# Layers 2 and 3 of a four-layer image kernel: the nine taps of each depthwise convolution tile shared out in another way among TensorE, VectorE, ScalarE and GpSimd

## The chip, the core and the metric

The kernel runs on one core of a Trainium2 chip. The metric is the device time of one execution in microseconds (us); lower is better. Before the change it is 25110.91 us, the median of three runs (25106.78 to 25119.97).

## What is computed

Eight images of 64 x 64 pixels with 192 channels go through four layers. Layer 0 is a state-space block with two depthwise convolutions, layer 1 a selective scan in four directions, and layers 2 and 3 are the same small block, which is the part that the change touches:

```
def _L2_conv_ref(x, w, b):            # layer 3 is the same with its own w and b
    out = jax.lax.conv_general_dilated(x, w, window_strides=(1, 1), padding='SAME', ...,
                                       dimension_numbers=('NHWC', 'HWIO', 'NHWC'), feature_group_count=C)
    return out + b
...
def _gn(v, G=32, eps=1e-5):
    ...
    m = jnp.mean(g, axis=(1, 2, 4), keepdims=True)
    s = jnp.var(g, axis=(1, 2, 4), keepdims=True)
    return ((g - m) / jnp.sqrt(s + eps)).reshape(v.shape)
```

Each of these layers normalises its input over groups of six channels of an image, runs a depthwise 3 x 3 convolution over it (nine taps, one weight for each tap and channel), adds a bias, and adds the result to the input. All arithmetic is float32.

## The kernel before

The program runs in three parts, one after another: layer 0 (function `layer0`), layer 1 (`layer1_in` and `layer1_scan`), and `tail`, which holds the end of layer 1 and layers 2 and 3. Data between the parts lies in DRAM. `tail` is the only part that changes.

**Tiling.** Channels lie on partitions, 192 of them as two groups (`ct`) of 96. The 4096 pixels of an image are cut into eight strips of eight rows, 512 pixels each. The unit of a convolution is a tile: one strip of one channel group, 96 x 512, so there are 16 tiles for each image and layer and 256 in the kernel. A tile's input, with one more row above and below, is loaded into the tile `x2` or `x3` (`load_rows`, L1249).

**Four threads.** `tail` is written as four generators, and `together` (L74) goes round them, running each up to its next `yield`. The order in which this writes instructions is the order of every engine's queue; nothing is reordered later.

- `sums` (L1138) loads the four direction outputs of a strip (`yin`, by SyncE's DMA queue, `fetch`, L1129) and adds them: L1142 and L1146 on VectorE, L1143 on GpSimd. Then it takes row statistics (L1151, L1152, L1154), a reciprocal root (L92 to L97, with a load of the activation table, L1156), and normalises on ScalarE (L1161).
- `project` (L1168) transposes a strip on TensorE (L1177, evicted by L1179), multiplies it by a gate (matmuls L1183, Silu L1191 with its table load, product L1193), projects it (matmuls L1201), adds the residual (L1203), takes statistics (L1204) and stores the strip as `x2`. ScalarE normalises its input (L695).
- `all_convolutions(2)` runs layer 2 and stores `x3`, and `all_convolutions(3)` runs layer 3 and stores the output. Layer 2 of an image needs the statistics of the whole image, so it starts when the eight strips of the projection are done, beside the projection of the next image; layer 3 lies another image behind. `affine` (L1210) makes the weights and biases of an image: the normalisation is folded into them, so that the centre tap also holds the residual's one, and `edge` corrects the first and the last pixel of each row, where a tap would fall outside the image.

**One tile before** (`convolve`, L1260). TensorE multiplies the input by five diagonal matrices, for taps 1, 4 and 7 (the centre column) and 3 and 5, into one PSUM bank (L1282). ScalarE evicts the bank with the bias into `y` in SBUF (L1292). VectorE adds the edge corrections (L1296, L1297) and the other four taps, one instruction each, multiplying `x` by the weight and adding to `y`, all in SBUF (L1303). For layer 2, VectorE then takes statistics (L1313) and the strip goes to `x3`. For layer 3, `turn` (L1319) transposes the strip on TensorE (L1329), ScalarE copies it (L1331), and it goes out; this is done after the first eviction of the next strip. The eight PSUM banks are two for transposes (`tp`), three for the projection (`mm`) and three for convolutions (`cv`).

Of the kernel before, what the change touches and what calls it, by code (L numbers as in the profile page):

```python
# [10 lines left out]
AF = mybir.ActivationFunctionType  # L11
ALU = mybir.AluOpType
# [3 lines left out]
B, H, W, C = 8, 64, 64, 192  # L16
L = H * W
CP, CT = 96, 2
# [7 lines left out]
NJ = 512  # L26
NCH = L // NJ
# [644 lines left out]
def layers123(ctx: ExitStack, tc, a, dr, x1, mv1, out, cst):  # L672
# [416 lines left out]
def tail(ctx: ExitStack, tc, a, load, w_in, normed, yk, x2, x3, out, cst):  # L1089


    nc = tc.nc
    ident, grp = cst[0], cst[4]
    IDC = ident[:CP, :CP]
    R, NB = NJ // W, NJ // 128
    wp = ctx.enter_context(tc.tile_pool(name="wt", bufs=1))
    pool = ctx.enter_context(tc.tile_pool(name="t1", bufs=2))
    psum = ctx.enter_context(tc.tile_pool(name="pt1", bufs=1, space=PSUM))

    def bank(tag):  # L1100
        return mk(psum, [128, NJ], tag, bufs={"tp": 2, "mm": 3, "cv": 3}[tag])

    onw, onb = load("onw", [DP, DT]), load("onb", [DP, DT])
    w_out = load("w_out1", [DP, DT, C])
    zero = mk(wp, [CP, W], "zero")
    nc.vector.memset(zero, 0.0)
    TAPS = (1, 4, 7, 3, 5)
    base = {}
    for i in (2, 3):
        w, bt = mk(wp, [CP, CT, 9], f"w{i}"), mk(wp, [CP, CT], f"b{i}")  # L1110
        nc.sync.dma_start(w, a[f"L{i}_w"])
        nc.sync.dma_start(bt, a[f"L{i}_b"])
        dg, ws = mk(wp, [CP, CT, len(TAPS), CP], f"dg{i}"), mk(wp, [CP, CT, 3], f"ws{i}")
        for ct in range(CT):
            for j, tap in enumerate(TAPS):
                nc.vector.tensor_scalar(dg[:, ct, j, :], IDC, w[:, ct, tap : tap + 1], None, ALU.mult)
# [2 lines left out]
            nc.vector.tensor_tensor(ws[:, ct, :], ws[:, ct, :], w[:, ct, 6:9], ALU.add)  # L1119
        base[i] = w, bt, dg, ws  # L1120
    strips = [(b, r) for b in range(B) for r in range(NCH)]
    yin, rows, halo, stats, par = {}, {}, {}, {}, {}
    done = {"sums": 0, "x2": 0, "x3": 0}

    def at(s):
        return 0 <= s < len(strips)
# [41 lines left out]
    def project(s):  # L1168
# [5 lines left out]
        for o in range(DT):  # L1174
            pt = bank("tp")
            for t in range(NB):
                nc.tensor.transpose(pt[:, t * 128 : (t + 1) * 128], v[:, t, o * 128 : (o + 1) * 128], ident)  # L1177
            yield
            nc.scalar.activation(yn[:, o, :], pt, AF.Identity, bias=onb[:, o : o + 1], scale=onw[:, o : o + 1])  # L1179
        for o in range(DT):  # L1180
            ps = bank("mm")
            for ct in range(CT):
                nc.tensor.matmul(  # L1183
                    ps,
                    w_in[:, ct, DIN + o * 128 : DIN + (o + 1) * 128],
                    gx[:, ct, :],
                    start=ct == 0,
                    stop=ct == CT - 1,
                )
# [20 lines left out]
    def affine(i, b):  # L1210
# [24 lines left out]
        wi, edge = mk(pool, [CP, CT, 9], f"wi{i}"), mk(pool, [CP, CT, 3], f"edge{i}")  # L1235
        dgi = mk(pool, [CP, CT, len(TAPS), CP], f"dgi{i}")
        for ct in range(CT):
# [11 lines left out]
    def load_rows(i, s):  # L1249

        if not at(s):
            return
        b, r = strips[s]
        t = halo[i, s] = mk(pool, [CP, CT, (R + 2) * W], f"x{i}")
        lo, hi = max(0, r * R - 1), min(H, (r + 1) * R + 1)
        d0 = lo - (r * R - 1)
        src = (x2 if i == 2 else x3)[b]
        nc.sync.dma_start(t[:, :, d0 * W : (d0 + hi - lo) * W], src[:, :, lo * W : hi * W])

    def convolve(i, s, before=None):  # L1260


        b, r = strips[s]
        gm, wi, edge, dgi, cb = par[i]
        x, y = halo.pop((i, s)), mk(pool, [CP, CT, NJ], f"y{i}")
        if i == 2 and r == 0:
            stats[3, b] = mk(pool, [CP, CT, NCH, 6], "st3")
        for ct in range(CT):
            for edge_row, at_row in ((0, 0), (NCH - 1, (R + 1) * W)):
                if r == edge_row:  # L1270
                    nc.scalar.activation(  # L1271
                        x[:, ct, at_row : at_row + W], zero, AF.Identity, bias=gm[:, ct : ct + 1]
                    )
        for ct in range(CT):
            ps = bank("cv")[:CP]
            sv = x[:, ct, :].rearrange("p (h w) -> p h w", w=W)
            pv = ps.rearrange("p (h w) -> p h w", w=W)
            yv = y[:, ct, :].rearrange("p (h w) -> p h w", w=W)
            for j, tap in enumerate(TAPS):
                dy, dx = tap // 3, tap % 3 - 1  # L1280
                w0, w1 = max(0, -dx), W - max(0, dx)
                nc.tensor.matmul(  # L1282
                    pv[:, :, w0:w1],
                    dgi[:, ct, j, :],
                    sv[:, dy : dy + R, w0 + dx : w1 + dx],
                    start=j == 0,
                    stop=j == len(TAPS) - 1,
                    skip_group_check=True,
                )
                if j % 2:  # L1290
                    yield
            nc.scalar.activation(y[:, ct, :], ps, AF.Identity, bias=cb[:, ct : ct + 1])  # L1292
            yield
            if ct == 0 and before is not None:
                yield from turn(*before)
            nc.vector.tensor_scalar(yv[:, :, 0:1], yv[:, :, 0:1], edge[:, ct, 0:1], None, ALU.add)  # L1296
            nc.vector.tensor_scalar(yv[:, :, W - 1 : W], yv[:, :, W - 1 : W], edge[:, ct, 2:3], None, ALU.add)  # L1297
            for tap in range(9):
                if tap in TAPS:
                    continue  # L1300
                dy, dx = tap // 3, tap % 3 - 1
                w0, w1 = max(0, -dx), W - max(0, dx)
                nc.vector.scalar_tensor_tensor(  # L1303
                    yv[:, :, w0:w1],
                    sv[:, dy : dy + R, w0 + dx : w1 + dx],
                    wi[:, ct, tap : tap + 1],
                    yv[:, :, w0:w1],
                    ALU.mult,
                    ALU.add,
                )  # L1310
                yield
            if i == 2:
                nc.vector.bn_stats(stats[3, b][:, ct, r, :], y[:, ct, :])  # L1313
        if i == 2:
            nc.sync.dma_start(x3[b][:, :, r * NJ : (r + 1) * NJ], y)
            done["x3"] = s + 1
        return y

    def turn(s, y):  # L1319

        b, r = strips[s]
        ot = mk(pool, [128, NB, C], "ot")
        for g in range(NB // 2):
            ps = bank("tp")
            for j in range(2):
                t = (2 * g + j) * 128
                for ct in range(CT):
                    c0 = j * C + ct * CP
                    nc.tensor.transpose(ps[:, c0 : c0 + CP], y[:, ct, t : t + 128], IDC)  # L1329
            yield  # L1330
            nc.scalar.copy(ot[:, 2 * g : 2 * g + 2, :], ps[:, 0 : 2 * C].rearrange("p (j c) -> p j c", j=2))  # L1331
        nc.sync.dma_start(out[b].rearrange("(g j p) c -> g p j c", p=128, j=NB)[r], ot)
# [15 lines left out]
            yield from project(s)  # L1348

    def all_convolutions(i):  # L1350
        before = None
        for s in range(n):
            b, r = strips[s]
            if r == 0:
                while done[f"x{i}"] < s + NCH:
                    yield
                load_rows(i, s)
                yield from affine(i, b)
            if r < NCH - 1:
                load_rows(i, s + 1)  # L1360
            y = yield from convolve(i, s, before)
            if i == 3:
                before = s, y
        if before:
            yield from turn(*before)
        yield

    with every_engine(tc):
        together(all_projections(), all_sums(), all_convolutions(2), all_convolutions(3))
# [83 lines left out]
```

## Time and profile before

| what | us |
| --- | --- |
| median of three runs (lowest to highest) | 25110.91 (25106.78 to 25119.97) |
| span of the profiled execution, first to last instruction | 25098.0 |
| of this, `tail`, from 22890 to the end | 2208 |
| PE busy over the whole span | 23784.2 (95%) |
| VectorE (DVE) busy | 22334.3 (89%) |
| ScalarE (ACT) busy | 20190.7 (80%) |
| GpSimd (POOL) busy | 17651.1 (70%) |

The profiler records one execution. Its page gives the span of that execution; the time of the same execution outside its span is not listed, so it is the 12.9 us between the span and the median of the runs that are taken for what lies around. Shares of busy time are averages over all parts; for a change in `tail`, the stages of `tail` have to be read by themselves. PE is TensorE's matmul stream and PEld its loading of weights, which overlaps it. "Idle before" is time in which an engine stood still ahead of an instruction, and the arrow names what ended it.

### The profile page before, as it was taken

To read this page: it belongs to the slowest core of one execution; us is meant where nothing else is said; L and a number is where in the kernel's file an instruction comes from. 1 tells how busy PE (TensorE), PEld (TensorE's weight loads), DVE (VectorE), ACT (ScalarE), POOL (GpSimd) and SP (SyncE) were. 2 spreads that over 40 slices of the span, in tenths; PEclk is the share of its full clock that TensorE was granted. 3 is DMA by queue.
4 is the path that set the end of the run, shared out by engine and by line. 5 is a ranking of instruction groups with operands and counts; after the bars stand their busy time and mean duration, and the time that the engine had idled before them with its cause. 6 is when DMAs were issued, how large, how long until landed. Compare 5 with 4: busy or idle time off the path is not lost.

```text
span 25098.0 us, 445961 instructions
## 1 busy us (share of the span) xinstructions
PE 23784.2 (95%) x156672; PEld 18458.1 (74%) x156672; DVE 22334.3 (89%) x26682; ACT 20190.7 (80%) x40488; POOL 17651.1 (70%) x18332
## 2 busy tenths in 40 slices
PE   8999999988899999999999999999999999998999
PEld 4444444445688888888888888888888888885333
DVE  6777777766799999999999999999999999998887
ACT  4555555544599999999999999999999999997443
POOL 2322322310399999999999999999999999995110
PEclk8888888899999999999999999999999999999999
DMA  1111111123333333333333333333333333335554
GB/s 59 47 43 46 46 47 43 38 70 114 110 100 95 96 101 95 95 103 95 95 101 97 95 99 98 95 97 100 95 95 104 95 95 102 95 95 157 170 175 122
DMA packets 1506272, 2337.12 MB, mean 93 GB/s; under 512 B 249997, under 2 KB 775949, under 8 KB 1504026
## 3 DMA queue, kind: packets, MB, share of 16 engines
q1 hardware_dynamic: 1496858, 2283.42, 31.5%
q8 instruction: 1236, 20.25, 0.3%
q0 software_dynamic: 7168, 25.17, 0.3%
q14 instruction: 1010, 8.27, 0.1%
HBM read 1847.54 MB, written 460.59 MB: 92 GB/s over the span
## 4 chain that ended last, share of the span: by engine, by line
PE 36%; ACT 31%; DVE 13%; POOL 13%; issue 6%; DMA 0%; POOLq 0%; SPq 0%; DVEq 0%; ACTq 0%
ACT dA L1003 13%; POOL hc L1053 11%; ACT sb L987 7%; PE pd L1009 6%; PE yt L942 5%; DVE h L1044 5%; ACT bd L987 4%; PE cv L1282 4%; PE y L592 3%; PE pd L1011 2%; PE mm L901 2%; PE fc L626 2%; PE y L519 1%; PE cv L774 1%; PE tp L564 1%
## 5 line engine op out<-in xcount | busy, mean ns | idle before, releaser
L1053 POOL TENSOR_TENSOR hc<-h,bc 128x512 f32<-128x512 f32 x12288 | 15431.9, 1289 | 475.6 <-DVE h L1044 341.2
L1044 DVE TENSOR_TENSOR_SCAN h<-dA,st,pd 128x512 f32<-128x512 f32 x10752 | 12949.5, 1262 | 530.1 <-PE pd L1009 374.4
L1003 ACT ACTIVATE dA<-dl,A_logs 128x512 f32<-128x512 f32 x12288 | 8817.1, 718 | 47.0 <-DVE h L1044 39.6
L942 PE MATMUL yt<-sq,hc 128*128 128x128 f32 x49152 | 7489.3, 275 | 200.1 <-POOL hc L1053 93.8
L1009 PE MATMUL pd<-bd,dut 128*128 128x128 f32 x49152 | 6581.4, 277 | 254.4 <-DVE h L1044 232.1
L1009 PEld LDWEIGHTS pd<-bd,dut 128*128 128x128 f32 x49152 | 5968.5, 192 | 609.9 <-PE yt L942 342.9
L942 PEld LDWEIGHTS yt<-sq,hc 128*128 128x128 f32 x49152 | 5669.7, 141 | 644.3 <-POOL hc L1053 624.4
L987 ACT ACTIVATE sb<-dut,xt 128x384 f32<-128x384 f32 x8192 | 4779.5, 609 | 1.1 <-DVE dut L928 1.0
L1011 PE MATMUL pd<-sq,sb 128*128 128x128 f32 x24576 | 3739.5, 275 | 8.5 <-DVE h L1044 0.4
L1011 PEld LDWEIGHTS pd<-sq,sb 128*128 128x128 f32 x24576 | 2823.6, 141 | 479.1 <-DVE dl L915 380.8
L987 ACT ACTIVATE bd<-sq,xt 128x128 f32<-128x128 f32 x8192 | 3026.3, 395 | 0.0
L1044 DVE TENSOR_TENSOR_SCAN h<-dA,pd 128x512 f32<-128x512 f32 x1536 | 1770.8, 1204 | 117.0 <-PE pd L1009 67.2
L1143 POOL TENSOR_TENSOR yin<-yin,yin 128x1536 f32<-128x1536 f32 x64 | 233.9, 3655 | 1635.1 <-DMA yin<-y 892.5
L1282 PE MATMUL cv<-x,dgi 96*96 96x512 f32 (+1 forms) x2560 | 1175.0, 595 | 9.3 <-ACT x L1271 9.1
L481 POOL TENSOR_TENSOR xdt<-xb,dtv 128x384 f32<-128x384 f32 x256 | 217.1, 848 | 1186.6 <-ACT xb L475 1186.6
L234 DVE SCALAR_TENSOR_TENSOR x<-xs,cpe_w,x 96x504 f32<-96x504 f32 (+1 forms) x1024 | 886.6, 866 | 31.8 <-ACT x L222 21.7
L784 DVE SCALAR_TENSOR_TENSOR u<-xa,conv_w,u 128x504 f32<-128x504 f32 x1152 | 850.1, 743 | 50.5 <-ACT u L776 12.5
L1282 PEld LDWEIGHTS cv<-x,dgi 96*96 96x96 f32 x2560 | 413.0, 164 | 638.2 <-issue 604.5
L901 PE MATMUL mm<-xs,w_dt 13*128 13x512 f32 x1536 | 863.0, 641 | 1.8 <-DVE dl L915 1.0
L1055 POOL COPY st<-h 128x3 f32<-128x3 f32 x4096 | 825.0, 201 | 0.0
L1303 DVE SCALAR_TENSOR_TENSOR y<-x,wi,y 96x504 f32<-96x504 f32 x1024 | 796.0, 796 | 17.7
L626 PE MATMUL fc<-ff,fc_w 128*96 128x512 f32 x1536 | 791.0, 621 | 2.7 <-DVE xo L629 2.7
(263 smaller groups left out, 26186.7 us busy)
## 6 DMA issues: line engine op xcount, KB each, us to landing
bc<-bcd SPq DMA_DIRECT2D x4096, 256.0 KB
yin<-y SPq DMA_DIRECT2D x256, 768.0 KB
csb<-csd SPq DMA_DIRECT2D x256, 384.0 KB
dut<-ut SPq DMA_DIRECT2D x128, 768.0 KB
y<-ys SPq DMA_DIRECT2D x128, 768.0 KB
dut<-ut SPq DMA_DIRECT2D x256, 384.0 KB
y<-ys SPq DMA_DIRECT2D x256, 384.0 KB
xt<-x1d SPq DMA_DIRECT2D x128, 384.0 KB
```

What stands on the lines that cost most here:

```text
L234: nc.vector.scalar_tensor_tensor(d[:, :, w0:w1], s[:, dy : dy + R, w0 + dx : w1 + dx], w[:, ct, tap : tap + 1], d[:, :, w0:w1], ALU.mult, ...
L626: nc.tensor.matmul(ps, f2w[:, o, ct * CP : (ct + 1) * CP], ff[:, o, :], start=o == 0, stop=o == 5)
L784: nc.vector.scalar_tensor_tensor(uv[:, o, :, w0:w1], tv[:, o, dy : dy + R, w0 + dx : w1 + dx], cw[:, o, tap : tap + 1], uv[:, o, :, w0:w1] ...
L901: nc.tensor.matmul(ps, w_dt[:, k, o * 128 : (o + 1) * 128], made["xs"][0 : 1 + R1, :], start=True, stop=True)
L942: nc.tensor.matmul(yt[:, t * 128 : (t + 1) * 128], src[:, t * 128 : (t + 1) * 128], mat, is_transpose=mat is ident, start=first and t == 0 ...
L987: nc.scalar.activation(v, src, AF.Copy, scale=m["xt"][:, t, 1 + R1 + n : 2 + R1 + n])
L1003: nc.scalar.activation(dA, ready[s]["dl"][:, o, :], AF.Exp, scale=aneg[:, k, o, n : n + 1])
L1009: nc.tensor.matmul(dst, ready[s]["dut"][:, t, cols], brows[g, t], start=True, stop=True)
L1011: nc.tensor.transpose(dst, brows[g, t][:, cols], ident)
L1044: nc.vector.tensor_tensor_scan(h[:, o, rev], decay.pop(j)[:, rev], turned.pop(j)[:, rev], 0.0 if first else st[:, o, n : n + 1], ALU.mult, ...
L1053: nc.gpsimd.tensor_tensor(hc, h[:, o, :], held[g], ALU.mult)
L1282: nc.tensor.matmul(pv[:, :, w0:w1], dgi[:, ct, j, :], sv[:, dy : dy + R, w0 + dx : w1 + dx], start=j == 0, stop=j == len(TAPS) - 1, skip_g ...
```

## The change

The nine taps of a tile are split into three columns. The centre column (taps 1, 4, 7) stays on TensorE, now in full rows of 512, as three matmuls. The left column (0, 3, 6) is added by VectorE directly in PSUM (`side`), before the eviction. The right column (2, 5, 8) is made by ScalarE as three products in SBUF (`product`, six buffers for each layer), and after the eviction GpSimd adds the three products and the two edge corrections to `y` (`add`, and the two `tensor_scalar`).

A tile now goes through three steps in a line: `new` (matmuls and products), `old` (left side in PSUM, eviction, GpSimd's adds) and `older` (statistics and store, or the turn). Each call of `step` handles three successive tiles at once, one in each stage. When the input of the next image isn't there yet, and at the end, the line is emptied with two empty steps. The banks become two for the projection and four for convolutions, the input tiles get three buffers, and the diagonals of taps 3 and 5 are no longer made.

```diff
-        return mk(psum, [128, NJ], tag, bufs={"tp": 2, "mm": 3, "cv": 3}[tag])
+        return mk(psum, [128, NJ], tag, bufs={"tp": 2, "mm": 2, "cv": 4}[tag])
...
-    TAPS = (1, 4, 7, 3, 5)
+    TAPS, BY_DVE, BY_POOL = (1, 4, 7), (0, 3, 6), (2, 5, 8)
...
-        t = halo[i, s] = mk(pool, [CP, CT, (R + 2) * W], f"x{i}")
+        t = halo[i, s] = mk(pool, [CP, CT, (R + 2) * W], f"x{i}", bufs=3)
...
-    def convolve(i, s, before=None):
...
+    def column(m, j):
+        if j == 0:
+            m["ps"] = bank("cv")[:CP]
+        nc.tensor.matmul(
+            m["ps"], m["dg"][:, j, :], m["x"][:, j * W : j * W + NJ], start=j == 0, stop=j == 2, skip_group_check=True
+        )
+
+    def product(m, tap):
+        v, src = reach(m, tap)
+        t = m[tap] = mk(pool, [CP, NJ], f"prod{m['i']}", bufs=6)
+        nc.scalar.activation(by_rows(t)[:, :, v], src, AF.Copy, scale=m["w"][:, tap : tap + 1])
+
+    def side(m, tap):
+        v, src = reach(m, tap)
+        u = by_rows(m["ps"])[:, :, v]
+        nc.vector.scalar_tensor_tensor(u, src, m["w"][:, tap : tap + 1], u, ALU.mult, ALU.add)
+
+    def add(m, tap):
+        v, _ = reach(m, tap)
+        u = by_rows(m["y"])[:, :, v]
+        nc.gpsimd.tensor_tensor(u, u, by_rows(m[tap])[:, :, v], ALU.add)
+
+    def step(i, new, old, older):
+
+        for j in range(3):
+            if new:
+                column(new, j)
+                product(new, BY_POOL[j])
+            if j:
                 yield
+            if old:
+                side(old, BY_DVE[j])
+        yield
+        if older and i == 2:
...
+            nc.vector.bn_stats(stats[3, b][:, older["ct"], r, :], older["y"])
+            if older["ct"] == CT - 1:
+                nc.sync.dma_start(x3[b][:, :, r * NJ : (r + 1) * NJ], ys.pop((i, older["s"])))
+                done["x3"] = older["s"] + 1
+        if older and i == 3 and older["ct"] == CT - 1:
+            yield from turn(older["s"], ys.pop((i, older["s"])))
+        yield
+        if old:
...
+            nc.scalar.activation(old["y"], old["ps"], AF.Identity, bias=old["bias"])
+        yield
+        if old:
+            for tap in BY_POOL:
+                add(old, tap)
+            for at_col, e in ((0, 0), (W - 1, 2)):
+                v = by_rows(old["y"])[:, :, at_col : at_col + 1]
+                nc.gpsimd.tensor_scalar(v, v, old["edge"][:, e : e + 1], None, ALU.add)
+        yield
...
     def all_convolutions(i):
-        before = None
+        line = [None, None]
+
+        def push(m):
+            yield from step(i, m, *line)
+            line.insert(0, m)
+            line.pop()
+
         for s in range(n):
             b, r = strips[s]
             if r == 0:
+                if done[f"x{i}"] < s + NCH:
+                    for _ in range(2):
+                        yield from push(None)
                 while done[f"x{i}"] < s + NCH:
                     yield
...
-            y = yield from convolve(i, s, before)
-            if i == 3:
-                before = s, y
-        if before:
-            yield from turn(*before)
+            for ct in range(CT):
+                yield from push(begin(i, s, ct))
+        for _ in range(2):
+            yield from push(None)
         yield
```

More of the change, by code (lines that the diff above doesn't have):

```diff
@@ L1121, in tail @@
     strips = [(b, r) for b in range(B) for r in range(NCH)]
-    yin, rows, halo, stats, par = {}, {}, {}, {}, {}
+    yin, rows, halo, stats, par, ys = {}, {}, {}, {}, {}, {}
     done = {"sums": 0, "x2": 0, "x3": 0}
@@ L1258, in load_rows, with reach, by_rows, begin @@
         nc.sync.dma_start(t[:, :, d0 * W : (d0 + hi - lo) * W], src[:, :, lo * W : hi * W])
-    def convolve(i, s, before=None):
+    def reach(m, tap):
+        dy, dx = tap // 3, tap % 3 - 1
+        w0, w1 = max(0, -dx), W - max(0, dx)
+        return slice(w0, w1), by_rows(m["x"])[:, dy : dy + R, w0 + dx : w1 + dx]
+    def by_rows(v):
+        return v.rearrange("p (h w) -> p h w", w=W)
+    def begin(i, s, ct):
         b, r = strips[s]
         gm, wi, edge, dgi, cb = par[i]
[L1265 to L1294, printed above, removed]
-                yield from turn(*before)
[L1296 to L1310, printed above, removed]
-                yield
[L1312 to L1317, printed above, removed]
@@ new lines, in begin @@
+        m = {"i": i, "s": s, "ct": ct, "x": halo[i, s][:, ct, :], "w": wi[:, ct, :]}
+        m["edge"], m["bias"], m["dg"] = edge[:, ct, :], cb[:, ct : ct + 1], dgi[:, ct, :, :]
+        for edge_row, at_row in ((0, 0), (NCH - 1, (R + 1) * W)):
+            if r == edge_row:
+                nc.scalar.activation(m["x"][:, at_row : at_row + W], zero, AF.Identity, bias=gm[:, ct : ct + 1])
+        return m
+    def column(m, j):
[4 more added lines that the diff above has]
+        )
@@ new lines, in step @@
+    def step(i, new, old, older):
[4 more added lines that the diff above has]
+            if j:
+                yield
+            if old:
+                side(old, BY_DVE[j])
+        yield
+        if older and i == 2:
+            b, r = strips[older["s"]]
+            if r == 0 and older["ct"] == 0:
+                stats[3, b] = mk(pool, [CP, CT, NCH, 6], "st3")
+            nc.vector.bn_stats(stats[3, b][:, older["ct"], r, :], older["y"])
[6 more added lines that the diff above has]
+        if old:
+            s, ct = old["s"], old["ct"]
+            if ct == 0:
+                ys[i, s] = mk(pool, [CP, CT, NJ], f"y{i}")
+            old["y"] = ys[i, s][:, ct, :]
+            nc.scalar.activation(old["y"], old["ps"], AF.Identity, bias=old["bias"])
[7 more added lines that the diff above has]
+        yield
@@ L1360, in all_convolutions @@
                 load_rows(i, s + 1)
-            y = yield from convolve(i, s, before)
-            if i == 3:
-                before = s, y
-        if before:
-            yield from turn(*before)
+            for ct in range(CT):
+                yield from push(begin(i, s, ct))
+        for _ in range(2):
+            yield from push(None)
         yield
```

## The prediction

> **What bounds the kernel now.** I read the page first (who is busy), then the busy time by stage (where the change can act), then the groups and the single lines (what one instruction costs).
>
> ```profile
> span 25098.0 us, 445961 instructions
> ```
>
> Only the last 2208 us, the tail, hold the changed code. Cut by stage (columns: window, its length, busy time of PE, PEld, DVE, ACT and POOL with their instruction counts, granted clock, DMA share, GB/s):
>
> ```profile
> 22890.00:23077.00 187.00, 121.61 (x316) 55.00 (x314) 131.98 (x244) 97.59 (x145) 44.49 (x13) 0.80 0.72 232
> 23077.00:23290.00 213.00, 186.91 (x495) 78.43 (x495) 188.07 (x361) 103.11 (x164) 28.58 (x8) 0.94 0.66 198
> 23290.00:24870.00 1580.00, 1464.33 (x4070) 625.11 (x4068) 1343.81 (x2639) 705.36 (x1144) 161.84 (x45) 0.96 0.56 166
> 24870.00:25006.00 136.00, 128.77 (x336) 51.37 (x336) 104.47 (x209) 27.49 (x49) 0.00 (x0) 0.96 0.31 86
> 25006.00:25098.00 92.00, 78.90 (x234) 33.19 (x234) 56.31 (x116) 21.77 (x43) 0.00 (x0) 0.91 0.25 72
> ```
>
> Stages: A, projection of image 0 alone; B, image 1 beside convolution 2 of image 0; C, six images, each beside 32 convolution tiles; D, both convolutions without projection; E, convolution 3 of the last image alone. In C, PE is busy 1464 of 1580 and DVE 1344, while ACT has 705 and POOL 162. So PE sets the pace, 263 us an image, and the change moves work to the two engines with room.
>
> The groups (line, engine, operation, count | busy, mean ns of one | idle before):
>
> ```profile
> L1282 PE MATMUL cv<-x,dgi 96*96 96x512 f32 (+1 forms) x2560 | 1175.0, 595 | 9.3 <-ACT x L1271 9.1
> L1303 DVE SCALAR_TENSOR_TENSOR y<-x,wi,y 96x504 f32<-96x504 f32 x1024 | 796.0, 796 | 17.7
> L1292 ACT ACTIVATE y<-cv,acb 96x512 f32<-96x512 f32 x256 | 173.8, 681 | 712.3 <-PE cv L1282 694.8 <-issue 6.7 <-DVE y L1303 5.4
> ```
>
> A matmul is two passes (2560 for 1280); ten passes take 4.26 us in the chain of waits, 0.427 each. Single lines (min/median/max ns):
>
> ```profile
> L1143 POOL TENSOR_TENSOR yin<-yin,yin x64: 3416/3437/5455, 22910.5 to 24756.5; 128x1536 f32<-128x1536 f32 x64
> ...
> L1053 POOL TENSOR_TENSOR hc<-h,bc x12288: 1253/1285/1382, 6680.6 to 22889.5; 128x512 f32<-128x512 f32 x199
> ...
> L97 DVE TENSOR_TENSOR rs<-rs_r,rs_t x64: 161/161/3309, 22922.9 to 24821.9; 128x4 f32<-128x4 f32 x64
> ...
> L1044 DVE TENSOR_TENSOR_SCAN h<-dA,st,pd x10752: 1243/1257/1283, 6742.5 to 22886.1; 128x512 f32<-128x512 f32 x200
> ```
>
> A four-element L97 of 0.161 us took up to 3.309, as long as a whole L1143: a VectorE operation with both inputs in SBUF waits until GpSimd's running one ends. The scan, with one input in PSUM, stays within 2% beside GpSimd that is busy all the time. So the new VectorE form, input and output in PSUM, should be free of this.
>
> **The sums per image in C** (32 tiles):
> - PE loses 4 of 10 passes: 32 x 4 x 0.427 = 55; 244 - 55 = 189.
> - DVE loses four L1303 (0.796) and the edges L1296 and L1297 (0.269 and 0.225) per tile: 32 x 3.68 = 118. It gains three PSUM sides. No row writes PSUM from VectorE: bounds 0.667 (L915, reads PSUM) and 1.257 (the scan); I take 0.74, the median of L1303, the same operation. 32 x 3 x 0.74 = 71; 224 - 118 + 71 = 177.
> - ACT gains three products per tile: between L987 (0.609 for 384 columns) and L1003 (0.718 for 512); I take 0.68. 118 + 32 x 3 x 0.68 = 183.
> - POOL gains three adds: (3437 - 1285) / 1024 = 2.1 ns a column, so 1.27 for 504; bounds L1053's minimum 1.253 and 1.706, the median of L610 (96x512) in layer 0. Two edge columns at 0.22, near the small copy L1055 (0.198); the upper bound is L543 (0.584, 384 columns). The five hang on one another; where L482 waits for L481, 0.09 lies between:
>
> ```profile
> 1013.45 0.89 POOL L481 TENSOR_TENSOR xdt<-xb,dtv 128x384 f32<-128x384 f32 x1
> 1014.43 1.03 POOL L482 TENSOR_TENSOR xw<-xdt,E 128x384 f32<-128x384 f32 x1
> ```
>
> So 3 x 1.27 + 2 x 0.22 + 4 x 0.09 = 4.6 a tile, 147 an image, 174 with the 27 of before.
>
> By busy time alone every engine is under 190, far below 263. The order decides.
>
> **The ring.** A product buffer comes free when GpSimd's add has read it, and six are two tiles. So products of tile k+1 wait for the adds of tile k-1, which wait for that tile's eviction, on the same ScalarE, just ahead in its queue. One turn: eviction 0.68, handover 0.07, three adds 3 x 1.27 + 2 x 0.09 = 3.99, handover 0.06, the last product 0.67: 5.5 us a tile, against 4.27 of PE before. What stands behind a waiting product on ScalarE is the projection's work: 11 us a strip (L1161, L1179, L1191, L695, two table loads, from the groups) and 0.9 of copies for the turn. PE's projection waits for these, VectorE for PE. Of the six rounds of a step, three lie under the adds, so I let half of the 12 be hidden: +6. Then the port: L1143's 3.44 stands in GpSimd's queue ahead of adds (I count 2), and VectorE keeps 6.5 a strip with both inputs in SBUF (L1142, L1146, three L1193, the small ones of the row statistics), which either wait for an add or hold one up (bounds 0 and 6.5 plus a wait of up to 1.27 for each of 11; I count 4, since GpSimd is busy some two thirds of the time): +6.
>
> So a strip with n tiles takes 5.5n + 12 us, and not less than 23.4 (stage A, 187 / 8). On ScalarE's queue of the changed kernel an image's strips finish 0, 3, 4, 5, 6, 5, 6, 3 tiles: 23.4 + 28.5 + 34 + 39.5 + 45 + 39.5 + 45 + 28.5 = 283, 20 more than 263. **C: +120.** B, with five strips of 3 and three of at most 1: 5 x 28.5 + 3 x 23.4 = 213: **0**. A is untouched.
>
> D: 29 tiles. Two threads in step share a turn (about 9.9 for two), out of step they pay 5.5 each; 5.2 x 29 + 10 for the affine = 161, against 136: **+25.** E: every second tile waits for the turn, which needs the edges (0.6), transposes and two copies: 6.9 instead of 5.5; 8 x 12.4 = 99, and fill 5, affine 7, and 14 from the last column to the end (sides 2.2, eviction 0.7, adds 4.6, turn 2.5, store 4): 125 against 92: **+33.**
>
> Costed at nothing: the third projection bank (PE has some 90 us of slack an image; without it, 192 waits of up to a Silu, 0.6, 115 in all); the stores of x3 and out, one or two steps later on SP's queue (x3 is read an image later, only E sees it); bn_stats and turns that wait for GpSimd's edges (DVE has 100 us of slack); the third x buffer (no idle time at L1282 or L1303 is put down to a DMA).
>
> The clock: with PE busy 65% of stage A the granted clock was 0.80; in C it would be busy 189 / 283 = 67%, so 189 / 0.80 = 236, still below 283. The Trainium skill (TensorE: Matmul & The Clock Gate, Part 1) halves the clock after one idle window of some 3.4 us; if that held throughout, PE would need 378 an image and bind again, C +690. Row A speaks for a part of that only, and I take the row.
>
> **Sum:** 120 + 0 + 25 + 33 = +178. Span 25098 + 178 = 25276; the median of the runs, 25110.9, lies 12.9 above the span, so **25289 us**.
>
> **Rivals.**
> 1. *Faster:* the two threads fill each other's waits and GpSimd alone sets C: 174 + 52 (8 x 6.5 for the port) = 226, 37 less than 263; 6 x -37 = -222, D 29 x 4.6 + 10 = 143 (+7), E +33: -182, 24929. For it: all busy sums are under 190. Against: nearly every product waits for an add, on one queue. It decides the sign from 253 an image downward (6 x 10 = 60, about what D and E lose). Chance 0.27.
> 2. *No change:* the port costs 2 instead of 6 and two thirds of the projection is hidden: 6 a strip less in seven strips would be 241 an image, and some of that gives 245 to 262: 6 x -18 + 58 = -50 to 6 x -1 + 58 = +52, so 25061 to 25163. Chance 0.13.
> 3. *Much slower:* GpSimd's add at 1.7 as in L610, or VectorE's PSUM side at 1.257: with 1.7 the ring is 1.3 longer a tile, 6 x 32 x 1.3 = 250, D and E 58 more: 25597. Against: L610 ran beside VectorE with two SBUF inputs. Chance 0.12.
>
> That the change does nothing is excluded: the queues hold three column matmuls a tile. The forecast keeps 0.48. Faster by over 0.2% (about what a measurement of this kernel can tell) 0.27, within 0.13, slower 0.60. Range 24930 to 25600, the two outer rivals; about 0.2 lies outside.
>
> **What would show it.** Right: in C, ACT idle ahead of products put down to POOL, adds near 1.27, PE some 65% busy, an image near 283. Wrong: adds above 1.5, sides above 0.9, C under 253, or waits of PE for the second bank.

## The result and the profile after

The changed kernel takes 25217.5 us (median of four runs, 25204.6 to 25222.0) against 25109.3 for the kernel before beside it: ratio 1.0043 [1.0028, 1.0057], so it is 108 us **slower**. The forecast was 25289 and slower; the sign and the mechanism held, the size was 72 us too large.

The first line of the page, and the stages of `tail` by busy time (window, length, then PE, PEld, DVE, ACT and POOL with their counts, granted clock, DMA share, GB/s):

```profile
span 25202.7 us, 445621 instructions
```

```profile
22885.00:23078.00 193.00, 126.28 (x326) 56.84 (x327) 134.48 (x259) 101.54 (x153) 35.72 (x12) 0.81 0.76 240
23078.00:23280.00 202.00, 158.11 (x385) 66.89 (x384) 149.69 (x265) 133.27 (x206) 122.32 (x97) 0.85 0.62 181
23280.00:24940.00 1660.00, 1285.41 (x3339) 542.61 (x3338) 1179.11 (x2096) 1096.07 (x1761) 1155.27 (x1017) 0.86 0.54 160
24940.00:25086.00 146.00, 98.69 (x209) 36.07 (x207) 67.06 (x99) 77.11 (x123) 121.52 (x140) 0.77 0.27 74
25086.00:25202.00 116.00, 69.16 (x164) 29.51 (x164) 39.55 (x73) 54.30 (x89) 69.58 (x80) 0.72 0.18 51
```

In C (third line) no engine is over 78% busy now; before, PE had 93%. The work was shared out evenly, and the stage became longer: that points to a chain of waits across engines. The groups of `tail` show where it is (busy, mean ns of one | idle before):

```profile
L1298 POOL TENSOR_TENSOR y<-y,prod 96x504 f32<-96x504 f32 x768 | 1114.9, 1452 | 620.2 <-ACT y L1327 579.8
L1281 PE MATMUL cv<-x,dgi 96*96 96x512 f32 x1536 | 811.3, 659 | 175.7 <-ACT x L1275 101.3 <-ACT y L1327 74.5
L1293 DVE SCALAR_TENSOR_TENSOR cv<-x,wi,cv 96x504 f32<-96x504 f32 x768 | 547.6, 733 | 70.2 <-PE cv L1281 57.5 <-issue 4.0
L1288 ACT ACTIVATE prod<-x,wi 96x504 f32<-96x504 f32 x768 | 526.7, 710 | 407.9 <-POOL y L1298 405.6
L1327 ACT ACTIVATE y<-cv,acb 96x512 f32<-96x512 f32 x256 | 170.8, 672 | 52.7 <-DVE cv L1293 52.7
L1334 POOL TENSOR_SCALAR y<-y,edge 96x8 f32<-96x8 f32 x512 | 173.7, 353 | 25.2
```

Read the first and the fourth line together: GpSimd's adds stood idle 580 us for the eviction on ScalarE (L1327), and ahead of its products ScalarE stood idle 406 us for adds (L1298). Each waits for the other, which is the ring of the forecast. The timeline of ScalarE in E, where nothing else runs, shows two of its turns (start, duration, instruction, in brackets the idle time ahead and what ended it):

```profile
25130.45 0.67 ACT L1327 ACTIVATE y<-cv,acb 96x512 f32<-96x512 f32 x1
25132.49 0.72 ACT L1288 ACTIVATE prod<-x,wi 96x504 f32<-96x504 f32 x1 [1.36 <-POOL y L1298]
25133.82 0.71 ACT L1288 ACTIVATE prod<-x,wi 96x504 f32<-96x504 f32 x1 [0.61 <-POOL y L1298]
25135.15 0.71 ACT L1288 ACTIVATE prod<-x,wi 96x504 f32<-96x504 f32 x1 [0.61 <-POOL y L1298]
25136.64 0.48 ACT L1349 COPY ot<-tp 128x384 f32<-128x384 f32 x1 [0.78 <-PE tp L1347]
25137.28 0.48 ACT L1349 COPY ot<-tp 128x384 f32<-128x384 f32 x1 [0.16 <-PE tp L1347]
25137.66 0.69 ACT L1327 ACTIVATE y<-cv,acb 96x512 f32<-96x512 f32 x1
...
25142.99 0.67 ACT L1327 ACTIVATE y<-cv,acb 96x512 f32<-96x512 f32 x1
```

The products start 1.33 us apart, the pace of the adds, and the next eviction stands behind the last of them. From eviction to eviction it is 7.21 us with the turn's copies and 5.33 without.

Stage lengths, from the start of each image's `affine` (L1218; C is the mean of six images, E runs to the end of the span). They are those of the one profiled execution of each kernel. Each ratio is to the kernel before as it ran beside that kernel, on the same chip (medians 25105 to 25116); the median in the first row belongs to the second row:

| kernel | median, us | ratio to before | B | C, an image | D | E |
| --- | --- | --- | --- | --- | --- | --- |
| before | 25109.3 | 1 | 214.4 | 263.1 | 141.4 | 93.8 |
| changed | 25217.5 | 1.0043 [1.0028, 1.0057] | 222.6 | 273.1 | 160.3 | 117.0 |
| e1_prod7 | 25165.2 | 1.0020 [1.0010, 1.0029] | 221.6 | 266.2 | 147.9 | 111.1 |
| e2_edges | 25221.3 | 1.0042 [1.0027, 1.0057] | 222.2 | 275.3 | 152.5 | 110.4 |
| e3_evac_first | 25267.9 | 1.0060 [1.0043, 1.0076] | 229.5 | 282.9 | 154.7 | 104.1 |
| e5_noadds | 24796.8 | 0.9873 [0.9858, 0.9888] | 198.3 | 226.3 | 95.4 | 63.8 |
| e6_zs_psum | 25210.0 | 1.0040 [1.0025, 1.0055] | 221.5 | 272.9 | 160.8 | 117.5 |
| e7_two_adds | 24985.7 | 0.9952 [0.9937, 0.9967] | 217.4 | 248.5 | 112.5 | 88.9 |
| e8_two_adds_4 | 25068.9 | 0.9984 [0.9975, 0.9994] | 217.4 | 258.6 | 128.0 | 95.0 |
| e9_sums_dve | 25228.7 | 1.0048 [1.0031, 1.0065] | 236.5 | 276.9 | 160.1 | 117.2 |
| e10_pe4 | 25025.8 | 0.9967 [0.9955, 0.9979] | 209.9 | 254.4 | 125.3 | 88.9 |
| e11_pe4_turn_last | 25004.0 | 0.9958 [0.9946, 0.9971] | 212.9 | 252.3 | 118.8 | 80.5 |
| e12_evac_first_sums | 25201.3 | 1.0037 [1.0023, 1.0050] | 233.8 | 275.0 | 154.5 | 104.1 |
| e13_two_adds_turn_last | 24987.9 | 0.9951 [0.9938, 0.9965] | 216.5 | 250.6 | 110.9 | 86.3 |

From the two profiled executions: up to the end of A -5.7, B +8.2, C +60.1 (six images), D +18.9, E +23.2, together +104.7, which is the difference of the spans (25202.7 - 25098.0). The end of A lies between 23053 and 23091 in the profiled executions of all these kernels, so a span by itself can be some tens of us off before the changed code starts; the stages and the medians are what is compared below.

### The profile page after: what moved, and what is told of

Same layout as the page of the kernel before. It is cut to its first block, busy times and chain, and to the rows that moved or that the text cites. A ratio compares the mean times of both kernels' runs of the same rounds, so it can differ in the third digit from the quotient of the medians.

```text
span 25202.7 us, 445621 instructions
## 1 busy us (share of the span) xinstructions
PE 23537.3 (93%) x155648; PEld 18348.1 (73%) x155648; DVE 22070.5 (88%) x25906; ACT 20694.7 (82%) x41277; POOL 18902.4 (75%) x19612
## 5 line engine op out<-in xcount | busy, mean ns | idle before, releaser
L1053 POOL TENSOR_TENSOR hc<-h,bc 128x512 f32<-128x512 f32 x12288 | 15406.9, 1285 | 483.0 <-DVE h L1044 342.6
L1003 ACT ACTIVATE dA<-dl,A_logs 128x512 f32<-128x512 f32 x12288 | 8833.0, 719 | 47.0 <-DVE h L1044 39.6
L1044 DVE TENSOR_TENSOR_SCAN h<-dA,pd 128x512 f32<-128x512 f32 x1536 | 1770.2, 1204 | 117.0 <-PE pd L1009 67.4
L1298 POOL TENSOR_TENSOR y<-y,prod 96x504 f32<-96x504 f32 x768 | 1114.9, 1452 | 620.2 <-ACT y L1327 579.8
L1281 PE MATMUL cv<-x,dgi 96*96 96x512 f32 x1536 | 811.3, 659 | 175.7 <-ACT x L1275 101.3
L784 DVE SCALAR_TENSOR_TENSOR u<-xa,conv_w,u 128x504 f32<-128x504 f32 x1152 | 850.0, 742 | 52.0 <-ACT u L776 13.9
L1288 ACT ACTIVATE prod<-x,wi 96x504 f32<-96x504 f32 x768 | 526.7, 710 | 407.9 <-POOL y L1298 405.6
```

The lines of the kernel that those rows point to most:

```text
L784: nc.vector.scalar_tensor_tensor(uv[:, o, :, w0:w1], tv[:, o, dy : dy + R, w0 + dx : w1 + dx], cw[:, o, tap : tap + 1], uv[:, o, :, w0:w1] ...
L1003: nc.scalar.activation(dA, ready[s]["dl"][:, o, :], AF.Exp, scale=aneg[:, k, o, n : n + 1])
L1044: nc.vector.tensor_tensor_scan(h[:, o, rev], decay.pop(j)[:, rev], turned.pop(j)[:, rev], 0.0 if first else st[:, o, n : n + 1], ALU.mult, ...
L1053: nc.gpsimd.tensor_tensor(hc, h[:, o, :], held[g], ALU.mult)
L1281: nc.tensor.matmul(m["ps"], m["dg"][:, j, :], m["x"][:, j * W : j * W + NJ], start=j == 0, stop=j == 2, skip_group_check=True)
L1298: nc.gpsimd.tensor_tensor(u, u, by_rows(m[tap])[:, :, v], ALU.add)
```

## The experiments

The theory is **the ring**: six product buffers are two tiles, so ScalarE's products wait for GpSimd's adds and hold up the very eviction that the next adds need. Its rival is **throughput**: GpSimd simply has too much to do, its adds stretched by VectorE's instructions with both inputs in SBUF (what the forecast calls the port), and buffers or order would not matter. A third candidate is the **place** of the eviction, behind statistics and turn.

**One more buffer.**

```diff
-        t = m[tap] = mk(pool, [CP, NJ], f"prod{m['i']}", bufs=6)
+        t = m[tap] = mk(pool, [CP, NJ], f"prod{m['i']}", bufs=7)
```

> One product buffer more for each layer (7 in place of 6), nothing else. The last product of a tile then waits for the second add of the tile two before, not the third. Ring theory (ScalarE's products wait for GpSimd's adds behind its own eviction): a turn is one add (1.3 us) shorter, so in stage E a plain step falls from 5.33 us to about GpSimd's own 4.5, and an image of stage C falls from 273 to about 255: some 25110 us. Port theory (the loss is GpSimd and VectorE shutting each other out of SBUF): the same instructions, so within 20 us of 25217. Bank theory (two projection banks in place of three make TensorE wait): within 20 us of 25217.

It took 25165: half of the loss is back, where all of it was expected. No engine's work changed, only when a product may be written. ScalarE's waits in C (engine, line, what it waited for: us in total, times, longest), first of the changed kernel, then of this one:

```profile
ACT prod L1288 <- POOL y L1298: 284.9, 210, 6.9
```

```profile
ACT prod L1288 <- POOL y L1298: 198.7, 109, 5.9
```

A third of the wait is gone and the number of waits is halved; C gains 6.9 us an image, D 12.4, E 5.9. Throughput alone doesn't allow that. With a seventh buffer the first product of a tile waits for the adds of a tile further back and the other two wait for one add fewer, so the ring is opened in part. Nine buffers, three whole tiles with all three adds, were not tried, so how much of the loss the ring accounts for in this kernel is not measured beyond that half.

**The edges on VectorE.** The two edge corrections go from GpSimd, after the eviction, to VectorE in PSUM, ahead of it.

```diff
+        if old:
+            for at_col, e in ((0, 0), (W - 1, 2)):
+                v = by_rows(old["ps"])[:, :, at_col : at_col + 1]
+                nc.vector.tensor_scalar(v, v, old["edge"][:, e : e + 1], None, ALU.add)
...
-                nc.gpsimd.tensor_scalar(v, v, old["edge"][:, e : e + 1], None, ALU.add)
```

> The two edge corrections move from GpSimd to VectorE, which adds them in PSUM ahead of the eviction. GpSimd loses 0.68 us a tile that lies outside the ring, except where the turn waits for it. Ring theory: stage E loses about 0.6 us in every second step (5 us in all), stage C little: 25180 to 25217 us. Throughput theory (GpSimd's busy time sets the pace): 32 tiles x 0.68 = 22 us an image, 160 us in all: about 25060 us.

25221, no change, though GpSimd lost 174 us of work. D and E gained 7.8 and 6.6 (the turn waits for the edges there), C lost 2.2 an image. The edges are not in the ring of products, so the ring expects little of them. The work is not gone but lies on VectorE, ahead of the eviction: evictions waited 79.5 us for it, against 52.7 for VectorE's sides before. But GpSimd's adds stood idle for evictions 764 us instead of 580; a GpSimd whose time sets the pace would not have traded its work for waiting.

**Eviction and adds first in the step**, ahead of the older tile's statistics, store and turn.

```diff
+        if old:
...
+            nc.scalar.activation(old["y"], old["ps"], AF.Identity, bias=old["bias"])
...
         if older and i == 2:
...
-        if old:
...
-            nc.scalar.activation(old["y"], old["ps"], AF.Identity, bias=old["bias"])
```

> Within a step, the eviction and the adds of a tile come ahead of the statistics, store or turn of the tile before. Ring theory: the turn's copies no longer stand ahead of the eviction on ScalarE, so in stage E the long steps (7.2 us) become like the short ones (5.3): 15 us; stage C gains where a turn stood in the ring, 2 to 8 us an image: 25150 to 25200 us in all. Port and bank theories: no change, within 20 us of 25217.

A **miss**: 25268, slower. E (-12.9) and D (-5.6) did what the ring says, C lost 9.8 us an image. One wait of VectorE in C shows why, first in the changed kernel, then with this edit (each over its own six images):

```profile
DVE yin L1146 <- POOL yin L1143: 69.4, 30, 2.7
```

```profile
DVE yin L1146 <- POOL yin L1143: 223.8, 36, 8.3
```

VectorE's sum L1146 waits up to 8.3 us for GpSimd's L1143, more than twice the 3.44 that L1143 takes: adds issued earlier now stand ahead of it. The projection would then start later and C be longer. Whether that is all of the loss was tested with e12 below.

**GpSimd's three adds left out** (`add(old, tap)` becomes `pass`). This kernel leaves a third of the convolution out of the output; its products are made and nobody reads them.

> GpSimd's three adds are left out (the products are made but not added; the edges stay), so a third of each convolution is missing from the output. No product waits for GpSimd any more. Ring theory: stage C falls from 273 us an image to 235 or less, D by about 35 and E by 35: about 24900 us, below the kernel before. If the loss is TensorE (fewer projection banks, a lower clock), stage C stays above 255 us an image and the whole above 25070 us.

24797: the adds cost 46.8 us an image in C (273.1 - 226.3), 65 in D and 53 in E. The products' waits vanish, and TensorE is 88% busy in C (1197.6 of 1356 us). Without the adds C is far below the 263 of before, so it is the adds and what waits for them that take the gain of the split back. This run doesn't tell the ring from GpSimd's work: both are gone in it.

**One source of the forecast's port less.** The Silu stays in PSUM, so VectorE's product L1193 has one input in SBUF instead of two.

```diff
-            nc.scalar.activation(zs[:, o, :], ps, AF.Silu)
+            nc.scalar.activation(ps, ps, AF.Silu)
...
-            nc.vector.tensor_tensor(zs[:, o, :], zs[:, o, :], yn[:, o, :], ALU.mult)
+            nc.vector.tensor_tensor(zs[:, o, :], ps, yn[:, o, :], ALU.mult)
```

> The projection's gate: ScalarE writes the Silu in place in PSUM, and VectorE multiplies it from there, so L1193 has one input in SBUF in place of two; nothing else differs from the changed kernel. Port theory (a VectorE operation with both inputs in SBUF and a GpSimd operation shut each other out): L1193's mean falls from 838 to about 680 ns, GpSimd's adds from a mean of 1452 ns to about 1400, and an image of stage C from 273 us to 262 to 268: 25150 to 25190 us. Ring theory alone, without the port: no change, within 15 us of 25217. A longer hold of the projection's two banks would show as more waiting of L1183, and a longer stage C.

The two groups of this kernel:

```profile
L1298 POOL TENSOR_TENSOR y<-y,prod 96x504 f32<-96x504 f32 x768 | 1084.6, 1412 | 650.2 <-ACT y L1327 609.5
L1193 DVE TENSOR_TENSOR zs<-mm,yn 128x512 f32<-128x512 f32 x192 | 130.9, 682 | 140.4 <-ACT mm L1191 139.6
```

L1193 went from 838 ns to 682 and the adds from 1452 to 1412, so the two do hold each other up; the time stayed (25210 against 25218, intervals overlapping). The 30 us that GpSimd saved turned into 30 us more of waiting for the eviction (609.5 against 579.8). The edit has a cost of its own, though, the one that the expectation names: the projection's banks are held longer, and L1183's matmuls stood idle 38.6 us ahead of them instead of 0.8, most of it in `affine`. So this run doesn't show that relief is worth nothing by itself.

**The last source on GpSimd's own queue.** L1143 goes to VectorE.

```diff
-        nc.gpsimd.tensor_tensor(y[2], y[2], y[3], ALU.add)
+        nc.vector.tensor_tensor(y[2], y[2], y[3], ALU.add)
```

> L1143, the sum of two direction outputs, moves from GpSimd's queue to VectorE; nothing else differs from the changed kernel. GpSimd loses 3.44 us a strip (27 an image), VectorE gains 1.74 a strip (14 an image). If L1143 stands in the ring as the forecast counted it (2 of 3.44 a strip, 16 an image): C falls from 273 to about 257 to 265 us, 25110 to 25170 us in all. If VectorE's loss eats this or L1143 lies in GpSimd's idle time: within 20 us of 25217, or above.

25229, not faster: C +3.8 an image, B +13.9. GpSimd lost 220 us of work and nothing came back; its adds stood idle for evictions 907 us instead of 580. That doesn't mean that L1143 lies in GpSimd's idle time. GpSimd's queue in C of the changed kernel (start, duration, instruction):

```profile
23672.80 0.60 POOL L1334 TENSOR_SCALAR y<-y,edge 96x8 f32<-96x8 f32 x2
23673.36 3.42 POOL L1143 TENSOR_TENSOR yin<-yin,yin 128x1536 f32<-128x1536 f32 x1
23676.74 5.31 POOL L1298 TENSOR_TENSOR y<-y,prod 96x504 f32<-96x504 f32 x3
```

The eviction that these three adds need had ended at 23667.6, so L1143 held them up for all of its 3.4 us. By the trace, 42 of the 192 tiles of C have an L1143 just ahead of their adds, and their adds start 7.7 us an image later for it, about 1 a strip. In e9 that is gone, but L1143 is now one more VectorE instruction with both inputs in SBUF: the adds' mean in C rises from 1487 ns to 1533, the edges' from 360 to 476, and evictions wait 79 us for VectorE instead of 53. One cost was exchanged for another.

**Two adds a tile.** Tap 5 goes to VectorE as a fourth side; two products and two adds a tile remain, and six buffers are now three tiles. Then the same with four buffers, that is two tiles again.

```diff
-    TAPS, BY_DVE, BY_POOL = (1, 4, 7), (0, 3, 6), (2, 5, 8)
+    TAPS, BY_DVE, BY_POOL = (1, 4, 7), (0, 3, 6, 5), (2, 8)
...
-                product(new, BY_POOL[j])
+                if j < 2:
+                    product(new, BY_POOL[j])
...
+        if old:
+            side(old, BY_DVE[3])
```

> Tap 5 moves from ScalarE and GpSimd to VectorE (four sides in PSUM, two products, two adds); the six product buffers now hold three tiles. Ring theory: products no longer wait for the adds of the eviction just ahead; ACT's waiting on POOL at the products goes to nearly nothing, and an image of stage C falls from 273 us towards the 226 of the run without adds: 235 to 245; stage E, where GpSimd has 3.2 us a tile and the turn's wait stays, near 85 us: 24930 to 25010 us, below the kernel before. If VectorE becomes the bound (four sides are 94 us an image, 200 in all), C stays above 250 and the whole above 25050 us.

```diff
-        t = m[tap] = mk(pool, [CP, NJ], f"prod{m['i']}", bufs=6)
+        t = m[tap] = mk(pool, [CP, NJ], f"prod{m['i']}", bufs=4)
```

> As e7_two_adds, but with four product buffers, two tiles as in the changed kernel: the same work as e7 with the ring closed, one add shorter. Ring theory: 10 to 15 us an image more than e7 in stage C, and ACT waits for POOL at the products: about 25040 to 25090 us. If only GpSimd's busy time matters and not the buffers, the same as e7 within 20 us.

24986 with six buffers and 25069 with four: **83 us, from buffers alone**, with the same instructions on every engine. That is the cleanest measure of the ring, in a kernel with two adds a tile. ScalarE's largest waits in C, with six and with four:

```profile
ACT zs L1191 <- PE mm L1183: 138.4, 72, 4.5
ACT yin L1161 <- DVE nm L1158: 106.3, 47, 3.9
ACT y L1330 <- DVE cv L1293: 98.5, 60, 8.7
```

```profile
ACT prod L1288 <- POOL y L1298: 227.2, 190, 4.6
ACT zs L1191 <- PE mm L1183: 124.6, 74, 4.6
```

With six, products hardly wait for GpSimd (1.3 us over the whole kernel); with four, that wait is the first again. Against the changed kernel, e8 is 149 us faster with the same two tiles of buffers: a turn of the ring has one add less, and GpSimd and ScalarE have less to do. These two are not told apart. e7 beats the changed kernel and the one before, by 0.48% [0.33, 0.63] of the latter. Evictions wait longer for VectorE in it, 141 us over `tail` against 53 in the changed kernel: there is a fourth side to wait for.

**The fourth tap on TensorE instead of VectorE**, and then layer 3's turn moved behind the adds.

```diff
-    TAPS, BY_DVE, BY_POOL = (1, 4, 7), (0, 3, 6), (2, 5, 8)
+    TAPS, BY_DVE, BY_POOL = (1, 4, 7, 5), (0, 3, 6), (2, 8)
...
+    def middle(m):
+        v, src = reach(m, 5)
+        nc.tensor.matmul(
+            by_rows(m["ps"])[:, :, v], m["dg"][:, 3, :], src, start=False, stop=True, skip_group_check=True
+        )
```

> As e7_two_adds, but tap 5 goes to TensorE as a fourth matmul (taps 1, 4, 7, 5) and VectorE keeps three sides; two products and two adds, six buffers, three tiles deep. In e7 the evictions waited 143 us for VectorE's sides; by busy time an image of stage C has TensorE 203 us (at a granted clock near 0.87 some 233), VectorE 177, ScalarE 161, GpSimd 140. If VectorE's fourth side is what holds e7 at 248.5 us an image, C falls to 238 to 245: 24920 to 24965 us, the fastest so far. If TensorE at its lower clock binds, C stays at 248 or more: 24985 us or above.

A **miss**: 25026, 40 above e7. C of this kernel, columns as in the stages above:

```profile
23290.00:24800.00 1510.00, 1352.13 (x3649) 566.55 (x3648) 1159.47 (x2037) 945.57 (x1533) 908.20 (x806) 0.92 0.58 174
```

PE is 90% busy at a granted clock of 0.92, and what waits for it waits longer than in e7: over C, the Silu (L1191) 185 us instead of 138, the residual's sum (L1203) 174 instead of 109. The evictions' wait for VectorE fell from 98 to 82. So what was saved on VectorE seems to be paid on TensorE; no run takes TensorE's part away to show it.

The second edit, on top of the first; e13 is the same edit on top of e7:

```diff
-        if older and i == 3 and older["ct"] == CT - 1:
-            yield from turn(older["s"], ys.pop((i, older["s"])))
...
             for tap in BY_POOL:
                 add(old, tap)
...
+        if older and i == 3 and older["ct"] == CT - 1:
+            yield from turn(older["s"], ys.pop((i, older["s"])))
```

> As e10_pe4, and in layer 3 alone the turn of a tile comes after the eviction and the adds of the next tile. e3_evac_first gained 13 us in stage E and 6 in D by this and lost 10 us an image in C. If that loss came from layer 2's adds ahead of L1143 in GpSimd's queue, this keeps the gain without the loss: 10 to 20 us below e10_pe4. If layer 3's turn is the cause, it is 20 to 60 us above e10_pe4.

25004, 22 less, as expected: the turn's copies no longer stand ahead of the eviction (D -6.5, E -8.3, C -2.1 an image).

> e7_two_adds (24986 us) with layer 3's turn after the eviction and the adds of the next tile, the difference that took e10 (25026) to e11 (25004), 22 us. The parts add up if the turn's wait and the ring are two separate costs: D and E fall by 6 and 8 us, C by up to 2 us an image: 24955 to 24975 us, below both kernels of the change and all others. If VectorE, later in e7 than in e10, takes the gain away: 24986 or above.

A **miss**: 24988, the same as e7. D and E gained 1.6 and 2.6, C lost 2.1 an image. The evictions of e7 and of this kernel:

```profile
L1330 ACT ACTIVATE y<-cv,acb 96x512 f32<-96x512 f32 x256 | 173.6, 679 | 142.8 <-DVE cv L1293 140.5 <-issue 0.9 <-ACT y L1330 0.7
```

```profile
L1328 ACT ACTIVATE y<-cv,acb 96x512 f32<-96x512 f32 x256 | 173.0, 676 | 221.8 <-DVE cv L1293 199.9 <-PE tp L1350 16.1 <-PE cv L1281 5.6
```

An eviction that comes earlier in ScalarE's queue only waits longer for VectorE's sides there (200 us against 141). The same move helps in e10, where the sides are three, and not here, where they are four.

**e3 again, with L1143 on VectorE**, to see whether e3 lost its time in GpSimd's queue (e3's edit and e9's together).

> e3_evac_first (25268 us, C 282.9 us an image) with L1143 on VectorE, as in e9_sums_dve (25229 us, C 276.9). In e3, VectorE waited 211 us of stage C for L1143, which stood behind adds in GpSimd's queue (69 us in the changed kernel). If this wait is e3's loss, it is gone here, and D and E are e3's: C 264 to 277, 25180 to 25220 us. If the loss has another cause (the order on ScalarE or TensorE), C stays near 283 to 287 and the whole near 25280 us.

25201 (the 211 us of the expectation and the 223.8 above are the same wait, over a shorter and over the whole of e3's C): C is 275.0, against 282.9 in e3 and 276.9 in e9, and D and E keep e3's gain (154.5, 104.1). With L1143 out of GpSimd's queue the early eviction costs nothing in C (275.0 against 276.9 without it), so e3's loss was L1143 standing behind adds.

## Why the prediction was right, and where its size was off

**The ring: right.** Same work and fewer buffers cost 83 us (e8 against e7); one more buffer gave half of the loss back (e1). A turn was forecast at 5.5 us and 6.9 with the turn's copies; E shows 5.33 and 7.21, 12.54 a strip against 12.4. What the runs leave open is the share: no run opens the ring fully and keeps all three adds.

**The mis-sized term: the length of a dense strip in C, 5.5n + 12.** Between starts of L695 in one image of C, the four strips of 5, 6, 5 and 6 tiles took 36.9 + 35.0 + 42.7 + 38.3 = 152.9. Forecast: 5.5 x 22 + 4 x 12 = 169. With 5.5 a tile kept, the constant is (152.9 - 121) / 4 = 8, but as a mean only: it would be 9.4, 2.0, 15.2 and 5.3 in the four strips, and strips of 6 tiles took less time than strips of 5. So the formula doesn't hold strip by strip. Which of its parts was too large can only be estimated:
- L1143 was counted with 2 of the +6 of the port. The trace has it ahead of waiting adds for about 1 a strip (above).
- VectorE's instructions with both inputs in SBUF were counted with 4. The adds have a mean of 1487 ns in C and 1250 in E, where no projection runs: 0.237 x 96 / 8 = 2.8 a strip that adds are stretched.
- These 3.8 for 6 would leave 4.2 for the other half, the projection's work on ScalarE, which was counted with 6.
- Or the 5.5 itself was too long. In D the forecast let two threads share a turn, about 9.9 us for two tiles, and D shows pairs of evictions 9.9 us apart (0.57 + 9.33, 3.98 + 5.90). In C both threads run too, and the forecast charged 5.5 for every tile. With 4.95 a tile the constant is (152.9 - 109) / 4 = 11, hardly below the forecast's 12.

No run separates these; e6 and e9, made to measure the port and L1143, each added a cost of its own.

**The light strips: too short in the mean.** In the same image the strips of 0, 3, 4 and 3 tiles took about 120, 114.4 forecast: the strip without a tile 30.5 instead of 23.4 and the one of 4 39.6 instead of 34, while one of the two strips of 3 took 22.1 instead of 28.5. In **B** (0 forecast, +8 measured) the two strips with at most one tile took 27.8 and 29.7, so there too 23.4 was too little for a strip that does little else.

**C** as a whole: 16 less in dense strips and 6 more in light ones make 273 for 283, six images +60 for +120. That the sum came so near is in part luck, since strips erred by up to 10 us in both directions. **D** +19 for +25: its length was forecast right (161, measured 160.3), but the 136 subtracted from it is a window that starts 7 us after D's `affine`; from L1218 on, D took 141.4 before. **E** +23 for +33: the eight strips were counted with 8 x 12.4 = 99, but from the first eviction (25100.0) to the last (25187.3) it is 87.2, and what lies around that took 30 for 26. All of the error of 72: C -60, B +8, D -6, E -10, and -6 up to the end of A, which the change doesn't touch; together -74 in the profiled executions.

**The prices.** Sides: 0.737 median (0.74 forecast), and not above 0.746 with adds running beside them, so VectorE's form in PSUM is free of GpSimd as argued. Products 0.710 (0.68). Adds 1.255 median (1.27), but 1.452 in the mean, and 1.487 in C, close to the 1.5 that was named as a sign of being wrong. Edges 0.314 median, 0.353 mean (0.22 taken, inside its bounds). PE was busy 214 us an image in C, not 189: its matmuls took longer (see the clock below), which the forecast covered by dividing 189 by 0.80: 236 was still below C.

**Costed at nothing.** The third projection bank: right, L1183's matmuls waited 0.7 us in all for a Silu. The statistics: VectorE waited 140.5 us in `tail` for the edges (L1315 for L1334), in an engine with 29% to spare in C; what it costs was not measured by itself.

**The clock.** Forecast 0.80 with PE 67% busy in C; measured 0.86 at 77% (1285 of 1660 us in the stage's line). L1183 shows what the figure is made of. Of its 576 matmuls in C, 416 took 591 to 699 ns, most of them 592; 118 took about 1061 and 15 about 1201; the mean in C rose from 625 to 723. So nearly all of them ran at either a high or a low speed. The Trainium skill (TensorE: Matmul & The Clock Gate, Part 1) names two such speeds, full and half; the groups here are 1.8 and 2.0 times apart, which agrees roughly. If the low one is half, an estimate from the granted clock is that it held for (1 - 0.86) / 0.5 = 28% of C. Halving throughout, which the forecast set aside, did not come.

**The rivals.** Rival 1 needed C under 253 and had 273: excluded. That GpSimd's time by itself sets the pace is excluded with it: it is 70% busy in C, and each time that work or stretching was taken off it (e2, e6, e9) its adds waited longer for evictions and the time stayed. Rival 2 (245 to 262 an image) was nearer than the forecast in size, by the median: its upper end of 25163 is 55 us below what was measured, the forecast 72 above. Its two assumptions were a smaller port, for which the trace speaks (3.8 for 6, by the estimate above), and more of the projection hidden, which no run shows by itself. Rival 3 is excluded by adds of 1.255 and sides of 0.737.

## What to carry to other kernels

Sharing work evenly among engines bought nothing here while two in-order queues waited for each other. Count how many units of work the buffers between them hold, and whether the producer's queue also carries the instruction that the consumer needs next. If so, one turn of that ring can be the pace, and room for another unit of work (three product tiles in flight instead of two, 83 us here) can be worth more than time taken off either engine. An instruction moved forward in a step moves ahead of others on every queue it uses; e3 lost 9.8 us an image to a sum on GpSimd (L1143) that nobody had counted as part of the edit. And an instruction that is moved off a queue is still somewhere: when an edit gains nothing, look whether its cost has turned up on another engine before calling what it removed free (e9).

## What the hardware showed that was not expected

- VectorE's multiply-add with input and output in PSUM and the other input in SBUF takes 668 to 746 ns for 96 x 504, no longer than the form all in SBUF (796 in the mean before, with single ones up to 3.962 us), and is not held by GpSimd's adds beside it.
- GpSimd's add of 1.255 us took up to 3.330 in C. VectorE's L1142, which has both inputs in SBUF, ran all of its 1.737 us within that add. Yet in e6, where adds were stretched 40 ns less, the time stayed.
- A GpSimd instruction on eight columns (L1334) costs 0.314 us, a quarter of the 1.255 that 504 columns take.
